# A mixture-of-experts kernel on one core: three partial sums instead of four, base rows loaded among the slots, and a row's transposes placed inside the prior row's products

## The chip, the core and the metric

The kernel runs on one core of one Trainium2 chip, as one launch. A core has engines with instruction queues of their own: TensorE (PE: matrix products and transposes; its weight loads are listed as PEld), VectorE (DVE), ScalarE (ACT), GpSimd (POOL) and SyncE (SP), whose queue here does nothing but issue DMAs. Each engine works through its queue in order and waits at an instruction whose inputs are not ready; what stands behind that instruction waits too. POOL issues the indirect DMAs, which scatter rows to addresses taken from an index. All DMAs share 16 DMA engines. TensorE's clock is granted: the profile gives it as a share of full speed, 0.50 or 1.00 here.

The metric is the device time of one execution in microseconds, the median over some runs. Lower is better.

## The reference, cut to what matters

The input is `x` (4 rows of 512 tokens, 512 channels each), a second tensor of the same shape and a small condition vector. Two blocks are added to `x`, one after the other:

```
x = x + attn(cond(x, side))          # recurrent mix, layer norms, dense products
x = x + ffn(cond2(x, side))
```

The part that the change touches is the end of the second block, a mixture of 32 experts. Each of the 2,048 tokens picks 8 experts and has a weight for each:

```
x_lat = x @ fc1_w.T                              # 256 values a token
h = relu2(einsum('tl,eil->eti', x_lat, w1))      # relu, then squared
h = h * cw.T[:, :, None]                         # 0 where the expert isn't picked
y_lat = einsum('eti,eli->tl', h, w2)             # sum over the experts
routed = y_lat @ fc2_w.T
shared = relu2(x @ shared_up_w.T) @ shared_down_w.T
return shared + routed
```

The kernel doesn't multiply all tokens by all experts. It sorts tokens by expert, works on groups of tokens of one expert, and adds each token's result into a row of a partial sum.

## The kernel before, in words

**Stages.** From the start to about 745 us the kernel computes the two conditioned mixes, the attention-like block, the router and the shared expert for the four rows, `b` = 0 to 3. At the end of that stage `base_dram[b]` holds, for each row, everything but the routed experts (`x`, the first block and the shared expert), channels on partitions: 4 chunks of 128 channels by 512 tokens. `x_dram` holds the tokens sorted by expert: per entry 256 latent values, the 32 weights and the token's number.

From 745 to about 1047 us run the **slots**: pairs of 128 entries each. `PAIRS` is 80; the first `SURE` = 74 always run, the rest under a condition, and in the profiled execution they do not run. The first `MIXED` = 16 pairs may hold two different experts, all later pairs hold 256 entries of one expert. For each pair, `fetch(i)` (L1068 to L1078) loads the entries with a DMA of SP, up to six pairs ahead; `slots(i, xg)` (L1117) transposes them on TensorE (`xt_ps`), multiplies by the expert's two matrices (`h_ps`, `y_ps`), scales by the token's weight on VectorE (`yo`, L1149) and adds the 128 x 256 results into DRAM with an indirect DMA that accumulates (L1151). Four arrays `sum_dram[0..3]` take these additions in turn, `(2 * i + j) % SUMS` for half `j` of pair `i`; two scatters into one array wait for each other. Entries that fill up a pair have weight 0 and go to spare rows behind row 2,047 of the array. The arrays are cleared by SP at 149 to 228 us from a block of zeros (`clear_sum`, L915 to L921), and the filling entries are laid out by `clear_tails` (L767).

From 1047 us to the end runs the **tail** (L1181 to L1219). For each row `b`:

- SP loads the row's part of each sum array (L1197), with token `t * 128 + p` on partition `p`, in runs of 1 KB;
- VectorE adds the four parts (L1203, three additions);
- TensorE transposes the result, eight 128 x 128 blocks into one PSUM tile `lt` (L1207);
- ScalarE copies it to SBUF as `yl` (L1211);
- TensorE multiplies by `fc2` in two halves, `j` = 0 and 1, four products each (L99), which the trace shows as eight matmuls;
- after each half VectorE adds the base (L1218), and SP stores the half to the output (L1219).

**What sets the order.** Each engine's instructions are written by hand inside a `manual_schedule` block for the engines it names; outside such a block, and for other engines, a scheduler picks the order. In the slots only VectorE is in written order. In the tail of the kernel before, no engine is: the scheduler orders all of it. SP is in written order up to the slots only, so the loads of base rows 0 to 2 (L1188) and of `fc2` (L1183), though written behind the slots, may be placed by the scheduler among the fetches.

Of the kernel before, what the change touches and what calls it, by code (L numbers as in the profile page):

```python
# [29 lines left out]
F32 = mybir.dt.float32  # L30
# [19 lines left out]
SURE = 74  # L50
MIXED = 16
WIDTH = 256 + E + 1
SUMS = 4
EXP30 = math.exp(30.0)
UNIT = NC * T

# [9 lines left out]
def model_kernel(ctx: ExitStack, tc: tile.TileContext, a: dict, out: bass.AP):  # L66
# [206 lines left out]

    x_dram = dram.tile([E * REGION + 3 * P, WIDTH], F32, tag="x_dram", name="x_dram")

    sum_dram = [dram.tile([ROWS + P, 256], F32, tag=f"sum{i}", name=f"sum{i}") for i in range(SUMS)]


    z_dram = [dram.tile([NC, P, T], F32, tag=f"z{b}", name=f"z{b}") for b in range(B)]
# [487 lines left out]
    def clear_tails():  # L767


        zeros = bp.tile([P, WIDTH], F32, tag="zeros", name="zeros")  # L770
        nc.vector.memset(zeros, 0.0)
        nc.gpsimd.iota(
            zeros[:, 256 + E : 257 + E], [[0, 1]], base=ROWS, channel_multiplier=1,
            allow_small_or_imprecise_dtypes=True,
        )
        for i in range(3):

            if i < 2:
                spare = x_dram[E * REGION : E * REGION + 2 * P, :].rearrange("(p j) n -> j p n", j=2)[i]
            else:  # L780
                spare = x_dram[E * REGION + 2 * P :, :]
            s = nc.gpsimd.dma_start(spare, zeros)
            tc.declare_no_dep(s.ins, group="scatter", reason="no two write one row")
            tc.add_to_no_dep_group("scatter", s.ins)
        yield
        ps = acc_tile()
        nc.tensor.matmul(ps[:1, 0, :E], lhsT=ones[:, 0:1], rhs=seen, start=True, stop=True)
        tail = bp.tile([1, E], F32, tag="tail", name="tail")
        nc.vector.tensor_tensor(tail, ps[:1, 0, :E], region[:1, :], ALU.add)
        ends = bp.tile([1, E], mybir.dt.int32, tag="ends", name="ends")  # L790
        nc.vector.tensor_scalar(ends, tail, -1.0, None, ALU.add)
        yield
        for e in range(E):
            _, (row,) = nc.values_load_multi_w_load_instructions(
                ends[0:1, e : e + 1], engines=[mybir.EngineType.SP], min_val=0, max_val=E * REGION,
                skip_runtime_bounds_check_because="a region has room for every row and a slot's tail",
            )
            s = nc.sync.dma_start(x_dram[bass.ds(row, P), :], zeros)
            tc.declare_no_dep(s.ins, group="scatter", reason="no two write one row but with zeros")
            tc.add_to_no_dep_group("scatter", s.ins)  # L800
            if e % 4 == 3:
                yield
# [112 lines left out]
    def clear_sum(i, j):  # L915

        s = sum_dram[i]
        if j < 2:
            nc.sync.dma_start(s[j * ROWS // 2 : (j + 1) * ROWS // 2, :].rearrange("(p r) n -> p (r n)", p=P), zero)
        else:  # L920
            nc.sync.dma_start(s[ROWS:, :], zero[:, :256])  # L921

    sums = iter([(i, j) for j in range(3) for i in range(SUMS)])

# [124 lines left out]
    with (  # L1049
# [19 lines left out]
        def fetch(i):  # L1069
            xg = ep.tile([P, 2, WIDTH], F32, tag="xg", name="xg", bufs=6)  # L1070
            rows = of_pair(2, i, ET.SP, E * REGION)
            if i < MIXED:
                for j, row in enumerate(rows):
                    nc.sync.dma_start(xg[:, j, :], x_dram[bass.ds(row, P), :])
            else:

                nc.sync.dma_start(xg, x_dram[bass.ds(rows[0], 2 * P), :].rearrange("(p j) n -> p j n", j=2))
            return xg  # L1078
# [37 lines left out]
        def slots(i, xg):  # L1116
            ps = turn(xg, "xt_ps")  # L1117
            xt = tile4("xt", [2, 2, P])
            if i < MIXED:
                nc.vector.tensor_copy(xt, ps)  # L1120
            else:
                nc.scalar.copy(xt, ps)

                w1 = tile4("w1", [2, 256])
                o = of_pair(0, i, ET.Activation, (E - 1) * (UNIT // 2))[0]
                nc.scalar.copy(w1.rearrange("p k n -> p (k n)"), big[:, bass.ds(o, 512)])  # L1126
            yield
            at = of_pair(0, i, ET.PE, (E - 1) * (UNIT // 2))
            h = tile4("ht", [2, 2, P])
            if i < MIXED:  # L1130
                ps = rows_times(xt, at, 0, "h_ps")
                r = tile4("hr", [2, 256])
                nc.scalar.activation(r, ps, AF.Relu)
                yield
                ps = turn(r, "ht_ps")
                nc.scalar.activation(h, ps, AF.Square)
            else:
                ps = inner(xt, w1)
                r = tile4("hr", [2, 256])
                nc.scalar.activation(r, ps.rearrange("p m j r -> p m (j r)"), AF.Relu)  # L1140
                yield
                nc.vector.tensor_tensor(h.rearrange("p m j r -> p m (j r)"), r, r, ALU.mult)  # L1142
            yield
            ps = rows_times(h, at, 1, "y_ps")
            y = tile4("yo", [2, 256], bufs=6)
            index = ep.tile([P, 2], mybir.dt.uint32, tag="index", name="index", bufs=9)
            nc.vector.tensor_copy(index, xg[:, :, 256 + E])
            for j, column in enumerate(of_pair(1, i, ET.DVE, 256 + E - 1)):
                nc.vector.tensor_scalar(y[:, j, :], ps[:, j, :], xg[:, j, bass.ds(column, 1)], None, ALU.mult)  # L1149

                nc.gpsimd.indirect_dma_start(  # L1151
                    out=sum_dram[(2 * i + j) % SUMS][:, :],
                    out_offset=bass.IndirectOffsetOnAxis(ap=index[:, j : j + 1], axis=0),
                    in_=y[:, j, :], in_offset=None,
                    bounds_check=ROWS + P - 1, compute_op=ALU.add,
                )
            yield

        def pairs(first, end):

            live = []
            with tc.manual_schedule(engines={ET.DVE}):
                for i in range(first, end + 3):
                    if i < end:
                        live.append(slots(i, fetch(i)))
                    for s in live:
                        next(s, None)
                    if len(live) > 3:
                        live.pop(0)
# [11 lines left out]

        fc2 = tile4("fc2", [2, C], bufs=1)
        nc.sync.dma_start(fc2, a["fc2"])  # L1183
        base = []
        for b in range(B):
            base.append(tile4(f"base{b}", [NC, T], bufs=1) if b + 1 < B else chunked(views(13, UNIT, 1)[0]))
            if b + 1 < B:
                nc.sync.dma_start(base[b], base_dram[b][:, :, :].rearrange("c p t -> p c t"))  # L1188
        got = Ring([v.rearrange("p (t n) -> p t n", t=NT) for v in views(1, NT * 256, 4 * SUMS)])
        lat_t = Ring([chunked(v, 2) for v in views(10, 2 * T, 2)])  # L1190
        res_ring = Ring([chunked(v, 2) for v in views(11, 2 * T, 4)])
        with tc.tile_pool(name="fpsum", bufs=2, space=bass.MemoryType.PSUM, reuse_waits="tile") as fps:
            for b in range(B):
                parts = []
                for s in sum_dram:
                    g = got()
                    nc.sync.dma_start(g, s[b * T : (b + 1) * T, :].rearrange("(t p) n -> p t n", p=P))  # L1197
                    parts.append(g)
                if b + 1 == B:
                    nc.sync.dma_start(base[b], base_dram[b][:, :, :].rearrange("c p t -> p c t"))  # L1200
                while len(parts) > 1:
                    for i in range(len(parts) // 2):
                        nc.vector.tensor_tensor(parts[i], parts[i], parts.pop(), ALU.add)  # L1203
                ps = fps.tile([P, 2, T], F32, tag="lt", name="lt")
                for t in range(NT):
                    for k in range(2):
                        nc.tensor.transpose(  # L1207
                            ps[:, k, t * P : (t + 1) * P], parts[0][:, t, k * P : (k + 1) * P], ident
                        )
                yl = lat_t()  # L1210
                nc.scalar.copy(yl, ps)  # L1211
                for j in range(2):
                    ps = fps.tile([P, 2, T], F32, tag="ps", name="ps")
                    for i in range(2):
                        o = (2 * j + i) * P
                        product(ps[:, i, :], lambda k: fc2[:, k, o : o + P], lambda k: yl[:, k, :], 2)
                    res = res_ring()
                    nc.vector.tensor_tensor(res, base[b][:, 2 * j : 2 * j + 2, :], ps, ALU.add)  # L1218
                    nc.sync.dma_start(out[b, 2 * j : 2 * j + 2].rearrange("c p t -> p c t"), res)  # L1219


# [40 lines left out]
```

## Time and profile before

| What | Value |
|---|---|
| median of 3 runs | 1114.19 us (1112.89 to 1116.45) |
| profiled execution, its own time | 1110.92 us |
| span of the profiled execution | 1109.2 us |
| mean granted TensorE clock | 0.983 |
| busy share: PE, DVE, ACT, POOL | 92%, 61%, 42%, 37% |
| scatters into the sums (L1151) | 148, mean 1610 ns on POOL, 4.0 us from issue to landing |
| loads of the sums (L1197) | 16 of 512 KB, 7.7 us from issue to landing |

The page divides the span into 40 slices of 27.7 us and gives a digit for the busy share of each, so the stages can be told apart in it. The timeline lists instructions in order of time: start, length, engine, line, operation, what is written and read, shapes, count, and in brackets how long the engine was idle before and what ended that. A time is counted from the start of the span. A "mean ns of one" is the time an instruction was in work; matmuls overlap, so the distance between two starts is the better measure for a row of them.

### The profile page before, as it was taken

How to read it: one execution, taken by the hardware profiler on the slowest of the kernel's cores; microseconds unless marked ns; L12 is line 12 of the kernel's file. 1: busy time of each engine (PE TensorE's matmuls, PEld its weight loads, DVE VectorE, ACT ScalarE, POOL GpSimd, SP SyncE). 2: the span in 40 equal slices, each digit the busy share in tenths (PEclk: the TensorE clock that was granted, in tenths of full speed). 3: DMA queues.
4: the chain of work that ended last, by engine and by line, in shares of the span. 5: the costliest groups of instructions: out<-in, count | busy, mean ns of one | idle time of the engine just before them, and what ended most of it. 6: DMA issues, size and time to landing. Idle time of an engine off the chain costs nothing.

```text
span 1109.2 us, 11550 instructions
## 1 busy us (share of the span) xinstructions
PE 1020.3 (92%) x3284; PEld 587.8 (53%) x3284; DVE 678.5 (61%) x1196; ACT 469.2 (42%) x671; POOL 408.3 (37%) x350
## 2 busy tenths in 40 slices
PE   3479899999999999999999999999999999999657
PEld 0134344344444444544454544448888888888523
DVE  7999799999896897439548622114434443333343
ACT  5555764865664655345235220303234444444100
POOL 3000000000001000436567635505777888888700
PEclk9989999999999999999999999999999999999869
DMA  3705384767347326754898859977988888888695
GB/s 131 274 29 209 114 246 164 306 175 228 132 100 241 146 104 184 253 141 131 257 332 276 258 184 291 284 231 183 202 137 143 143 142 144 144 148 148 68 287 205
DMA packets 105913, 208.41 MB, mean 188 GB/s; under 512 B 10837, under 2 KB 55385, under 8 KB 101177
## 3 DMA queue, kind: packets, MB, share of 16 engines
q1 hardware_dynamic: 71576, 152.07, 41.3%
q0 software_dynamic: 33728, 54.53, 27.3%
q10 hardware_dynamic: 544, 1.05, 0.2%
q8 instruction: 29, 0.48, 0.2%
q14 instruction: 36, 0.29, 0.1%
HBM read 126.87 MB, written 84.94 MB: 191 GB/s over the span
## 4 chain that ended last, share of the span: by engine, by line
PE 49%; DVE 25%; DMA 8%; issue 7%; ACT 6%; POOL 3%; SPq 0%; DVEq 0%; POOLq 0%; ACTq 0%
PE ps L99 17%; PE y_ps L1099 11%; PE h_ps L1110 9%; PE ps L500 6%; PE xt_ps L1088 3%; POOL x_dram L683 2%; PE h_ps L1099 2%; DMA big<-base 2%; DVE big L369 2%; DVE side L353 2%; DMA base<-big 2%; DVE big L353 2%; DVE side L369 2%; DVE big L465 2%; DMA sum<-yo,index 2%
## 5 line engine op out<-in xcount | busy, mean ns | idle before, releaser
L500 PE MATMUL ps<-big 128*128 128x512 f32 x896 | 392.6, 598 | 18.4 <-DVE big L465 7.9
L500 PEld LDWEIGHTS ps<-big 128*128 128x128 f32 x896 | 170.9, 192 | 236.4 <-issue 211.6
L1151 POOL DMA_INDIRECT sum<-yo,index x148 | 238.3, 1610 | 96.9 <-DVE yo L1149 73.0
L1149 DVE TENSOR_SCALAR yo<-y_ps,xg 128x256 f32<-128x256 f32 x148 | 64.8, 480 | 149.0 <-PE y_ps L1099 149.0
L683 POOL DMA_INDIRECT x_dram<-lat,index x128 | 139.5, 1090 | 42.6 <-issue 33.2
L1099 PE MATMUL y_ps<-big,ht 128*128 x592 | 140.3, 380 | 1.6 <-DVE ht L1142 1.6
L536 POOL DMA_DIRECT2D base<-big x8 | 10.6, 1323 | 313.6 <-DVE big L530 194.2
L1099 PEld LDWEIGHTS y_ps<-big,ht 128*128 128x128 f32 x592 | 106.8, 190 | 13.6 <-DVE ht L1142 2.2
L99 PE MATMUL ps<-big,sw 128*128 128x512 f32 x256 | 112.0, 593 | 0.2 <-DVE big L754 0.2
L1110 PE MATMUL h_ps<-xt,w 128*128 128x256 f32 x464 | 109.6, 379 | 0.0
L1110 PEld LDWEIGHTS h_ps<-xt,w 128*128 128x128 f32 x464 | 88.2, 190 | 11.8
L1140 ACT ACTIVATE hr<-h_ps 128x512 f32<-128x512 f32 x58 | 34.6, 597 | 132.0 <-PE h_ps L1110 132.0
L99 PEld LDWEIGHTS ps<-big,sw 128*128 128x128 f32 x256 | 48.4, 190 | 59.2 <-issue 57.6
L461 ACT ACTIVATE big<-big,vec,prior_g 128x511 f32<-128x511 f32 x80 | 58.4, 802 | 27.8 <-DVE big L454 27.8
L374 ACT ACTIVATE side<-side,tiny 128x512 f32<-128x512 f32 x32 | 23.1, 721 | 103.6 <-DVE side L371 103.5
L99 PE MATMUL ps<-sh,sw 128*128 128x512 f32 x128 | 56.7, 595 | 0.9 <-ACT sh L743 0.9
L465 DVE SCALAR_TENSOR_TENSOR big<-big,own_g 128x512 f32<-128x512 f32 x80 | 55.8, 749 | 0.3
L754 DVE TENSOR_TENSOR big<-big,ps 128x1024 f32<-128x1024 f32 x10 | 12.2, 1220 | 60.3 <-PE ps L99 36.6
L1126 ACT COPY w<-big 128x512 f32 x58 | 36.1, 622 | 28.3 <-DVE xt L1120 27.8
L369 DVE TENSOR_TENSOR_SCAN side<-decay,side 128x512 f32<-128x512 f32 x32 | 38.9, 1217 | 14.1 <-ACT side L354 14.1
L1088 PE MATMUL xt_ps<-ident,xg 128*128 128x128 f32 x296 | 44.3, 273 | 0.0
L1088 PEld LDWEIGHTS xt_ps<-ident,xg 128*128 128x128 f32 x296 | 36.9, 141 | 7.7 <-issue 0.5
(236 smaller groups left out, 1267.6 us busy)
## 6 DMA issues: line engine op xcount, KB each, us to landing
xg<-x_dram SPq DMA_DIRECT2D x58, 289.0 KB, 3.1
big<-in_w SPq DMA_DIRECT2D x32, 512.0 KB, 9.0
ekx<-side SPq DMA_DIRECT2D x16, 512.0 KB, 3.5
base<-big POOLq DMA_DIRECT2D x8, 1024.0 KB, 9.5
sum<-big SPq DMA_DIRECT2D x8, 1024.0 KB, 9.3
side<-ekx SPq DMA_DIRECT2D x16, 512.0 KB, 6.2
big<-sum SPq DMA_DIRECT2D x16, 512.0 KB, 7.7
side<-in_side SPq DMA_DIRECT2D x22, 256.0 KB, 6.6
```

The lines of the kernel that those rows point to most:

```text
L99: done[0] = nc.tensor.matmul(dst, lhsT=lhs(k), rhs=rhs(k), start=(k == 0), stop=(k == n - 1))
L353: nc.vector.tensor_tensor_scan(f, decb, data, 0.0, ALU.mult, ALU.add)
L369: nc.vector.tensor_tensor_scan(f[:, ::-1], decb, f[:, ::-1], 0.0, ALU.mult, ALU.add)
L461: nc.scalar.activation(m[:, c, 1:], xc[:, c, : T - 1], AF.Identity, bias=col(f"L0_attn_{which}_b", c), scale=prior_g[mu][:, c : c + 1],)
L465: nc.vector.scalar_tensor_tensor(m[:, c, :], xc[:, c, :], own_g[mu][:, c : c + 1], m[:, c, :], ALU.mult, ALU.add)
L500: done[0] = nc.tensor.matmul(ps[:, i, :], lhsT=w[:, k, f * P : (f + 1) * P], rhs=m[:, k, :], start=(k == 0), stop=(k == NC - 1),)
L683: s = nc.gpsimd.indirect_dma_start(out=x_dram[:, :], out_offset=bass.IndirectOffsetOnAxis(ap=index[:, i : i + 1], axis=0), in_=lats[:, t, ...
L1088: nc.tensor.transpose(ps[:, k, j, :], src[:, j, k * P : (k + 1) * P], ident)
L1099: nc.tensor.matmul(ps[:, j, :], lhsT=src[:, k, j, :], rhs=weights(at[j], of, k), start=(k == 0), stop=(k == 1),)
L1110: nc.tensor.matmul(ps[:, m, :, :], lhsT=w[:, k, m * P : (m + 1) * P], rhs=src[:, k, :, :], start=(k == 0), stop=(k == 1),)
L1149: nc.vector.tensor_scalar(y[:, j, :], ps[:, j, :], xg[:, j, bass.ds(column, 1)], None, ALU.mult)
L1151: nc.gpsimd.indirect_dma_start(out=sum_dram[(2 * i + j) % SUMS][:, :], out_offset=bass.IndirectOffsetOnAxis(ap=index[:, j : j + 1], axis=0 ...
```

## The change

Five things are changed.

- `SUMS` goes from 4 to 3. In the mixed pairs the halves still take the arrays in turn. From pair 16 on, both halves of pair `i` go to array `i % 3`, and the two scatters of one pair no longer wait for each other, since they hold different tokens of one expert. So that filling entries of one pair never meet in one row, the spare area of each array grows from 128 to 256 rows, and one of the spare blocks of entries gets row numbers 128 higher (`other`).
- The base rows are loaded in halves (512 KB each) by `load_base`, which is called among the pairs: seven halves there, the eighth with the loads of the sums.
- The sums are loaded with four tokens per partition: token `p * 4 + t` on partition `p`, one run of 4 KB per partition. All loads of all rows are written ahead of the arithmetic. ScalarE's copy puts the tokens back in order: it writes with a step of four elements.
- The tail's arithmetic is in a `manual_schedule` block for TensorE and VectorE. Additions, transposes and copy of a row are in `turned(b)`, which is called for row `b + 1` between the two halves of row `b`.
- The very last output half is added and stored in two pieces.

The diff, cut to its core:

```diff
-SUMS = 4
+SUMS = 3
...
-    sum_dram = [dram.tile([ROWS + P, 256], F32, tag=f"sum{i}", name=f"sum{i}") for i in range(SUMS)]
+    sum_dram = [dram.tile([ROWS + 2 * P, 256], F32, tag=f"sum{i}", name=f"sum{i}") for i in range(SUMS)]
...
+        other = bp.tile([P, 1], F32, tag="other", name="other")
+        nc.gpsimd.iota(
+            other, [[0, 1]], base=ROWS + P, channel_multiplier=1, allow_small_or_imprecise_dtypes=True,
+        )
...
-            s = nc.gpsimd.dma_start(spare, zeros)
...
+            parts = [(spare, zeros)]
+            if i == 1:
+                parts = [(spare[:, : 256 + E], zeros[:, : 256 + E]), (spare[:, 256 + E :], other)]
+            for dst, src in parts:
+                s = nc.gpsimd.dma_start(dst, src)
...
-            nc.sync.dma_start(s[ROWS:, :], zero[:, :256])
+            nc.sync.dma_start(s[ROWS:, :].rearrange("(p r) n -> p (r n)", p=P), zero[:, :512])
...
-                nc.gpsimd.indirect_dma_start(
-                    out=sum_dram[(2 * i + j) % SUMS][:, :],
+                s = nc.gpsimd.indirect_dma_start(
+                    out=sum_dram[(2 * i + j if i < MIXED else i) % SUMS][:, :],
...
+                if i >= MIXED:
+                    tc.declare_no_dep(s.ins, group=f"pair{i}", reason="rows of one expert")
+                    tc.add_to_no_dep_group(f"pair{i}", s.ins)
...
+        base = [[None, None] for _ in range(B)]
+        early = [(b, j) for b in range(B) for j in range(2)]
+
+        def load_base(b, j):
+
+            late = (b, j) == (B - 1, 1)
+            base[b][j] = chunked(views(13, 2 * T, 1)[0], 2) if late else tile4(f"base{b}{j}", [2, T], bufs=1)
+            nc.sync.dma_start(base[b][j], base_dram[b][halves[j]].rearrange("c p t -> p c t"))
...
+                    if i > MIXED and i % 4 == 0 and early:
+                        load_base(*early.pop(0)) if len(early) > 1 else None
...
-                    nc.sync.dma_start(g, s[b * T : (b + 1) * T, :].rearrange("(t p) n -> p t n", p=P))
+                    nc.sync.dma_start(g, s[b * T : (b + 1) * T, :].rearrange("(p t) n -> p t n", t=NT))
                     parts.append(g)
                 if b + 1 == B:
-                    nc.sync.dma_start(base[b], base_dram[b][:, :, :].rearrange("c p t -> p c t"))
+                    load_base(b, 1)
+
+            def turned(b):
+
+                parts = rows[b]
                 while len(parts) > 1:
                     for i in range(len(parts) // 2):
                         nc.vector.tensor_tensor(parts[i], parts[i], parts.pop(), ALU.add)
...
                 yl = lat_t()
-                nc.scalar.copy(yl, ps)
...
+                nc.scalar.copy(
+                    yl.rearrange("q k (p t) -> q k t p", t=NT), ps.rearrange("q k (t p) -> q k t p", t=NT)
+                )
+                return yl
+
+            with tc.manual_schedule(engines={ET.PE, ET.DVE}):
+                coming = turned(0)
+                for b in range(B):
+                    yl = coming
+                    for j in range(2):
+                        if j == 1 and b + 1 < B:
+                            coming = turned(b + 1)
+                        ps = fps.tile([P, 2, T], F32, tag="ps", name="ps")
+                        for i in range(2):
+                            o = (2 * j + i) * P
+                            product(ps[:, i, :], lambda k: fc2[:, k, o : o + P], lambda k: yl[:, k, :], 2)
+                        res = res_ring()
+
+                        for s in ((0, 1), (1, 2)) if (b, j) == (B - 1, 1) else ((0, 2),):
+                            s = slice(*s)
+                            nc.vector.tensor_tensor(res[:, s, :], base[b][j][:, s, :], ps[:, s, :], ALU.add)
+                            o = slice(2 * j + s.start, 2 * j + s.stop)
+                            nc.sync.dma_start(out[b, o].rearrange("c p t -> p c t"), res[:, s, :])
```

## The prediction

> **What bounds the kernel now.** I read the slices first, to see where TensorE is not full; then the timeline of the slots and of the tail; then the windows around the tail, for the clock; last the DMA issues.
>
> ```profile
> PE   3479899999999999999999999999999999999657
> PEclk9989999999999999999999999999999999999869
> ```
>
> TensorE is busy nine tenths or more from slice 6 to slice 37, and its clock is below nine tenths only in slice 3 and in slices 38 and 39. In the slots (745 to 1047 us) the timeline repeats a pair every 3.89 us with TensorE never idle: 220.00 us busy in 820 to 1040. No other engine's saving counts there. What remains is the tail:
>
> ```profile
> 1048.77 1.56 POOL L1151 DMA_INDIRECT sum<-yo,index  x1 [0.30 <-issue]
> 1053.81 12.96 SPq L1197 DMA_DIRECT2D big<-sum  x12
> 1060.70 1.22 DVE L1203 TENSOR_TENSOR big<-big 128x1024 f32<-128x1024 f32 x1 [14.59 <-DMA big<-sum]
> 1062.09 2.48 DVE L1203 TENSOR_TENSOR big<-big 128x1024 f32<-128x1024 f32 x2 [0.17 <-DMA big<-sum]
> 1064.72 1.94 PE L1207 MATMUL lt<-ident,big 128*128 128x128 f32 x8 [19.52 <-DVE big L1203]
> 1067.82 8.85 PE L99 MATMUL ps<-big,fc 128*128 128x512 f32 x16 [1.16 <-ACT big L1211]
> ...
> 1087.81 7.13 PE L99 MATMUL ps<-big,fc 128*128 128x512 f32 x16 [1.16 <-ACT big L1211]
> ...
> 1094.78 1.04 PE L1207 MATMUL lt<-ident,big 128*128 128x128 f32 x8
> ...
> 1095.91 1.01 ACT L1211 COPY big<-lt 128x1024 f32<-128x1024 f32 x1 [8.15 <-PE lt L1207]
> ...
> 1096.98 7.13 PE L99 MATMUL ps<-big,fc 128*128 128x512 f32 x16 [1.16 <-ACT big L1211]
> ...
> 1100.72 1.22 DVE L1218 TENSOR_TENSOR big<-big,ps 128x1024 f32<-128x1024 f32 x1 [4.51 <-PE ps L99]
> ...
> 1104.15 1.22 DVE L1218 TENSOR_TENSOR big<-big,ps 128x1024 f32<-128x1024 f32 x1 [2.21 <-PE ps L99]
> ```
>
> The reader is to see a head, a rhythm and an end. The head runs from the last scatter to the first transposes. The rhythm is one row per 9.17 us (1087.81 to 1096.98): 6.97 of products, 1.13 of transposes, 1.01 of ScalarE's copy, 0.06 to start. DVE's sums of the next row lie beside the products, ahead of the output adds, so TensorE waits only for the copy. The end is the last add, its store and the tail of the span (1104.15 to 1109.2).
>
> The third reading is the clock:
>
> ```profile
> 1040.60:1044.00 3.40, 1.83 (x9) 1.29 (x8) 1.55 (x4) 0.00 (x0) 2.79 (x3) 1.00 0.56 54
> 1044.00:1047.40 3.40, 1.20 (x6) 0.72 (x4) 0.88 (x2) 0.00 (x0) 2.79 (x3) 1.00 0.68 77
> 1047.40:1064.50 17.10, 0.00 (x0) 0.00 (x0) 3.60 (x3) 0.00 (x0) 2.62 (x2) 0.50 0.80 208
> 1064.50:1067.90 3.40, 2.02 (x9) 1.65 (x9) 1.29 (x2) 1.01 (x1) 0.00 (x0) 0.50 1.09 349
> 1067.90:1071.30 3.40, 3.40 (x4) 1.43 (x5) 2.46 (x3) 0.00 (x0) 0.00 (x0) 0.50 1.09 348
> 1071.30:1104.10 32.80, 29.39 (x85) 13.78 (x83) 15.54 (x13) 3.04 (x3) 0.00 (x0) 1.00 0.68 230
> ```
>
> Columns: the stretch, its length, busy time of PE, PEld, DVE, ACT, POOL, granted clock, DMA share, GB/s. The clock moves in steps of 3.41 us. A step with 1.83 us of matmuls (54%) leaves it full; one with 1.20 us (35%) is followed by half clock; 59% at half clock doesn't bring it back, a full step does.
>
> **The change, part by part.**
>
> *Base rows.* In the trace the scheduler already loads rows 0 to 2 (L1188, 1 MB each) at 766, 770 and 774 us, during the slots; only row 3's load is late (1084.06), and its first user waits for TensorE at 1100.72, not for it. So nothing is removed. In the compiled order of the changed kernel, seven halves go ahead of the seventh to ninth fetch on SP's queue. Fetches behind them wait at most 3.5 MB, some 10 us at the 348 GB/s of the tail. The seventh fetch is needed six pairs after the first, at 4.33 us each (760.25 to 764.58 on POOL). Cost: 0; without that cover, up to 10 us, once.
>
> *Three sums in the slots.* From pair 16 on a scatter waits for the scatters of three pairs before, at least 9.8 us after their issue (three pairs of 3.89 less the 1.86 between a pair's two); before it was 7.8. Scatters land 4.0 us after issue (median; 8.0 at most), so the wait is covered. In the 16 mixed pairs the distance falls from four scatters to three, some 6.2 us (4.33 + 1.87): covered at the median, short by 1.8 at the longest. GpSimd idles 0.9 us per mixed pair and `yo` has six buffers, so TensorE doesn't see it. POOL's backlog at the end of the slots is 1.2 us (the last product's first half is scaled by 1045.7, so two scatters of 1.56 with 0.30 between could end at 1049.1, and end at 1050.3). It may go or stay: minus 1.2 to 0, and I take 0. The spare-row edit adds one iota and one small DMA on POOL's queue before its first base add at 140 us, with idle time behind it: 0. Nine clears instead of twelve on SP: 0, for TensorE waits on VectorE there; half a microsecond either way stays in the range.
>
> *The head.* Four loads of 512 KB become three, in 4 KB runs instead of 1 KB. The first load landed 3.74 us after its issue, the next ones some 1.48 us apart (seen in 1063.63 and 1065.10, the landings of the fifth and sixth), so the third landed near 1060.6 and the fourth near 1062.0: the two DVE starts above. The longer runs cost a little less: 4 KB packets took 173 ns on an engine (the ekx loads), 16 engines, so 1.38 us a load. Third load: 1053.81 + 3.65 + 2 x 1.38 = 1060.2. Two dependent adds are 2.48, plus 0.1 and 0.12 to start: transposes at 1062.9 instead of 1064.7. Gain **1.8**.
>
> *The row turned between the halves.* This is the step that decides. The block has VectorE and TensorE in written order, and the code writes product, output add of half 0, then `turned(b + 1)` with its sums, then product of half 1. So on VectorE the next row's two sums stand behind an add that waits for the product of half 0, and on TensorE the transposes that wait for these sums stand ahead of half 1's product. TensorE now waits inside every row but the last. From a product's start: 3.74 to its output add (1096.98 to 1100.72), 1.22 for the add, 2.48 for the two sums, 0.15 to the transposes, 0.86 for eight of them (four take 0.43 from 833.34 to the next product at 833.77), 3.43 for half 1 (sixteen matmuls take 6.86, 704.05 to 710.91): 11.9 us to the next row's product. ScalarE's copy and its 0.06 are now beside half 1's product; without that cover they would be 1.1 more. Three rows: 3 x (11.9 - 9.17) = **8.1 lost**. What disappears per row is the copy gap of 1.1 and one sum that was hidden anyway; what is new is 4.2 us of idle TensorE.
>
> *The clock in these gaps.* A gap of 4.2 us, however it lies on steps of 3.41, puts at least 2.1 idle us into one of them: 39% busy or less. The row above dropped at 35% and held at 54%, so I take a drop in each of the three gaps. Then half clock lasts until a step is nearly full. Placing the gap at every phase of the step, 1.7 to 3.1 us of work time is lost per drop, 2.1 in the mean: 3 x 2.1 = **6.3 lost** (an estimate from the rows above). The Trainium skill ("TensorE: Matmul & The Clock Gate", What's actually happening) is milder: the clock halves after an idle window of about 3.4 us, free-running. A gap of 4.2 contains a whole one in about a quarter of the placings: less than one drop, 2 us in all. By the rule the sum below would be +7, by the row +11.6; I follow the row, since the 35% step was no idle window and dropped.
>
> *The strided copy.* ScalarE writes `yl` with a step of four elements. No row shows such a write; the nearest is the same copy, contiguous, 1.01 us. The skill's page "SBUF — State Buffer" (Door 1) speaks against it: accesses that move to a new 16-byte line pay a penalty, and a step of four fp32 values moves every time. It gives no time. Bounds: 1.01 and twice that. Only row 0's copy is on the path; the others have 3.43 us of product over them. I take 0, and 1.0 as the other end.
>
> *The end.* The last output add is split. The first half can start after the first two of four products, so the piece behind the last product is 128x512: 0.68 us (L1142's row) instead of 1.22, and its store is 256 KB instead of 512 (2.79 us to landing before, perhaps 0.5 less). Gain **1.0**.
>
> Sum: 8.1 + 6.3 - 1.8 - 1.0 = **+11.6 us**. On the profiled execution (1109.2 span, 1110.92 with what lies around it) that gives 1122.5. The three runs shown have a median of 1114.19, 3.3 above the profiled one; on it, **1125.8**.
>
> **Rivals.**
> *The clock holds in the gaps.* For it: the skill's rule; against: the 35% step. 8.1 - 1.8 - 1.0 = +5.3: 1119.5, or 1121.5 with one drop.
> *More is late.* The strided copy at double time (+1.0), a scatter wait in the mixed pairs (+1.8) or three drops at the costly phase (+3): 1128 to 1131.
> *Faster.* The turn is truly hidden: if the sums of the next row ended before half 0's product, a row would take 6.86 + 0.86 = 7.7 and the sum would be 3 x (7.7 - 9.17) - 1.8 - 1.0 = -7.2: 1107. The point is whether two sums fit ahead of the output add on VectorE; data would be there (six loads by 1064.4). The written order speaks against it.
> *The change doesn't do what it says* holds for the base rows, as shown; it is inside the main case.
>
> **Chances.** Main case 0.66 (its own range 1122 to 1129), clock holds 0.19, more is late 0.11, hidden 0.04. About 0.3% (3.3 us) is what a measurement can tell from no change. Same takes a small part of the second case, where POOL's backlog goes too (8.1 - 2.8 - 1.2 = +4.1) and the runs spread: 0.05. Range 1118.5 to 1130.
>
> **What would show it.** Between halves of a row, TensorE idle about 4 us, released by the sums; VectorE's order output add, sum, sum; the clock at 0.5 after these gaps; first transposes near 1063; slots at 3.89 us per pair. It is wrong if the sums of row 1 start before half 0's output add, or if the slots' pace moves.

## The result, and the profile after

The changed kernel takes **1125.44 us** (median of 4 runs, 1123.18 to 1126.34); the kernel before, run beside it, takes 1113.54 (4 runs, 1111.98 to 1116.45). The ratio is 1.0096 with a 95% interval of 1.0078 to 1.0115: 11.9 us slower, where 11.6 was forecast.

The profiled execution of the changed kernel took 1125.58 us, its span is 1123.8, its mean clock 0.978. These are the slices of its page, first TensorE's busy share and then the granted clock:

```profile
PE   3579899999999999999999999999999999999267
PEclk9989999999999999999999999999999999999779
```

The last three slices tell it: TensorE is busy two, six and seven tenths there (six, five and seven before), and the clock is at seven, seven and nine (eight, six and nine before). The timeline shows why, from TensorE's last product of the slots on:

```profile
1044.96 1.99 PE L1108 MATMUL y_ps<-big,ht 128*128 x8 [1.57 <-DVE ht L1151]
...
1052.39 1.56 POOL L1161 DMA_INDIRECT sum<-yo,index  x1 [0.31 <-issue]
1057.19 7.90 SPq L1220 DMA_DIRECT2D big<-sum  x12
1063.60 2.48 DVE L1230 TENSOR_TENSOR big<-big 128x1024 f32<-128x1024 f32 x2 [15.73 <-DMA big<-sum]
...
1066.23 1.94 PE L1234 MATMUL lt<-ident,big 128*128 128x128 f32 x8 [19.28 <-DVE big L1230]
1068.27 1.95 ACT L1238 COPY big<-lt 128x1024 f32<-128x1024 f32 x1 [26.08 <-PE lt L1234]
1070.27 6.18 PE L99 MATMUL ps<-big,fc 128*128 128x512 f32 x8 [2.10 <-ACT big L1238]
1076.49 1.22 DVE L1259 TENSOR_TENSOR big<-base,ps 128x1024 f32<-128x1024 f32 x1 [10.41 <-PE ps L99]
1077.63 2.48 DVE L1230 TENSOR_TENSOR big<-big 128x1024 f32<-128x1024 f32 x2
...
1080.25 1.94 PE L1234 MATMUL lt<-ident,big 128*128 128x128 f32 x8 [3.80 <-DVE big L1230]
1081.98 8.80 PE L99 MATMUL ps<-big,fc 128*128 128x512 f32 x16
...
1090.82 1.22 DVE L1259 TENSOR_TENSOR big<-base,ps 128x1024 f32<-128x1024 f32 x1 [2.21 <-PE ps L99]
1091.96 2.48 DVE L1230 TENSOR_TENSOR big<-big 128x1024 f32<-128x1024 f32 x2
1094.49 1.09 PE L1234 MATMUL lt<-ident,big 128*128 128x128 f32 x8 [3.71 <-DVE big L1230]
...
1107.86 1.09 PE L1234 MATMUL lt<-ident,big 128*128 128x128 f32 x8 [3.71 <-DVE big L1230]
...
1115.86 1.22 DVE L1259 TENSOR_TENSOR big<-base,ps 128x1024 f32<-128x1024 f32 x1 [2.21 <-PE ps L99]
1119.29 1.29 DVE L1259 TENSOR_TENSOR big<-big,ps 128x512 f32<-128x512 f32 x2 [2.21 <-PE ps L99]
```

Read the 1076.49 line and the two below it: output add, then the next row's two sums, then TensorE's transposes, which waited 3.80 us for them. The same triple stands at 1090.82 and before 1107.86. The output adds of the four first halves start at 1076.49, 1090.82, 1104.18 and 1115.86: distances of 14.33, 13.36 and 11.67, where before all three were near 9.15.

Two of the three rows are longer than the third, though the instructions are the same. The windows of the clock's steps say why (columns as in the prediction; the last three numbers are granted clock, DMA share and GB/s):

```profile
1075.30:1078.70 3.40, 1.15 (x3) 0.19 (x1) 2.21 (x2) 0.00 (x0) 0.00 (x0) 1.00 0.12 43
1078.70:1082.10 3.40, 1.85 (x9) 1.88 (x10) 1.37 (x2) 0.00 (x0) 0.00 (x0) 0.50 0.40 149
1092.40:1095.80 3.40, 1.31 (x9) 1.12 (x10) 2.00 (x2) 0.13 (x1) 0.00 (x0) 1.00 0.41 154
1095.80:1099.20 3.40, 3.40 (x5) 1.35 (x4) 0.00 (x0) 1.85 (x1) 0.00 (x0) 0.50 0.02 5
1102.60:1106.00 3.40, 1.55 (x4) 0.38 (x2) 1.81 (x2) 0.00 (x0) 0.00 (x0) 1.00 0.41 154
1106.00:1109.40 3.40, 1.54 (x10) 1.31 (x11) 1.77 (x2) 0.36 (x1) 0.00 (x0) 1.00 0.41 154
1109.40:1112.80 3.40, 3.40 (x9) 1.49 (x9) 0.38 (x1) 1.64 (x1) 0.00 (x0) 1.00 0.00 0
```

The first gap leaves its step 34% busy (1.15 of 3.40) and the next step runs at half clock; the second leaves 39% and the clock drops again. The third gap falls across a boundary: 46% and 45%, and the clock holds.

The two spans differ by 14.6 us. The table goes stage by stage. Of the kernel before, these are the last slot product and the first output add; the other lines stand in the prediction:

```profile
1043.20 2.00 PE L1099 MATMUL y_ps<-big,ht 128*128 x8 [1.57 <-DVE ht L1142]
...
1073.28 1.22 DVE L1218 TENSOR_TENSOR big<-base,ps 128x1024 f32<-128x1024 f32 x1 [2.61 <-PE ps L99]
```

| stage | before, us | after, us | difference |
|---|---|---|---|
| span's start to the end of the last slot product | 1045.20 | 1046.95 | +1.75 |
| from there to the first load of the sums | 8.61 | 10.24 | +1.63 |
| first load to first transposes | 10.91 | 9.04 | -1.87 |
| first transposes to first product | 3.10 | 4.04 | +0.94 |
| first product to its output add | 5.46 | 6.22 | +0.76 |
| that add to the last row's first add | 27.44 | 39.37 | +11.93 |
| last row's first add to the span's end | 8.43 | 7.95 | -0.48 |

The first row is not shown to be the change's. The difference is there at the first pair's transposes (745.25 before, 747.19 after). Ahead of them the diff touches only the clears of the sums and the entries that fill up pairs, and in experiments that share all of this with the changed kernel the transposes start at 745.36, 747.03 and 749.02, so executions scatter by more than the difference. The other rows sum to 12.9. The medians differ by 11.9; the profiled execution of before was 2.6 us below its median, and the profiles do not say in which stage.

The second row was not foreseen, and has a cause of its own. GpSimd's part of the timeline, in the mixed pairs and around pair 16:

```profile
762.00 1.56 POOL L1161 DMA_INDIRECT sum<-yo,index  x1 [0.85 <-DVE yo L1158]
...
766.96 1.55 POOL L1161 DMA_INDIRECT sum<-yo,index  x1 [3.40 <-DMA sum<-yo,index]
...
824.51 1.56 POOL L1161 DMA_INDIRECT sum<-yo,index  x1 [0.30 <-issue]
...
830.35 1.56 POOL L1161 DMA_INDIRECT sum<-yo,index  x1 [4.29 <-DVE yo L1158]
832.21 1.56 POOL L1161 DMA_INDIRECT sum<-yo,index  x1 [0.30 <-issue]
```

The scatter at 824.51 is the last mixed one, number 31, and goes to array 31 % 3 = 1. The next is pair 16's first, and goes to array 16 % 3 = 1. So it stands behind a scatter that was issued one place earlier, which landed at 828.32. GpSimd sat idle for 4.29 us; the VectorE instruction named as releaser had ended at 826.26, so the likely cause is the other wait, the landing (an experiment below tests it). The wait at 766.96 is of the kind that the prediction had priced, and that backlog was gone by pair 10. The one at pair 16 was not: a pair's first scatter then started 4.1 us after its data was ready, and still 3.1 at the last pair (1.2 before).

### The profile page after: what moved, and what is told of

It is laid out like the page before. It is cut to its first block, busy times and chain, and to the rows that moved or that the text cites. A ratio compares the mean times of both kernels' runs of the same rounds, so it can differ in the third digit from the quotient of the medians.

```text
span 1123.8 us, 11489 instructions
## 1 busy us (share of the span) xinstructions
PE 1025.7 (91%) x3284; PEld 589.2 (52%) x3284; DVE 668.8 (60%) x1193; ACT 473.6 (42%) x671; POOL 407.6 (36%) x352
## 5 line engine op out<-in xcount | busy, mean ns | idle before, releaser
L1119 PEld LDWEIGHTS h_ps<-xt,w 128*128 128x128 f32 x464 | 88.1, 190 | 11.9
```

The source lines that it names most:

```text
L1119: nc.tensor.matmul(ps[:, m, :, :], lhsT=w[:, k, m * P : (m + 1) * P], rhs=src[:, k, :, :], start=(k == 0), stop=(k == 1),)
```

## The experiments

The theory at this point: the written order costs 3 x 11.67 - 27.44 = 7.6 us, the two drops of the clock 39.37 - 3 x 11.67 = 4.4, pair 16's array 1.6, the strided copy 0.9, and the head and the end give 2.35 back. The rivals: the gaps come from late data, not from the order; the clock is slower for another reason than the gaps; the late scatters come from three arrays as such, or from the base loads. Four kernels ran on one chip, beside 11 runs of the kernel before (median 1113.40, 1111.19 to 1116.82).

**The sums ahead of the output adds.** Only VectorE's written order is changed: each row's sums stand before the adds that they were queued behind.

```diff
-            def turned(b):
+            def summed(b):
                 parts = rows[b]
                 while len(parts) > 1:
...
+            def turned(b):
+                parts = rows[b]
...
+                summed(0)
+                summed(1)
                 coming = turned(0)
...
                             nc.sync.dma_start(out[b, o].rearrange("c p t -> p c t"), res[:, s, :])
+                        if j == 0 and b + 2 < B:
+                            summed(b + 2)
```

> Only VectorE's order in the tail is moved: the two sums of row 1 stand ahead of row 0's first output add, those of rows 2 and 3 one half of a row earlier than in the changed kernel. Theory (the sums behind the output add make TensorE wait, and the gaps halve its clock): no gap at the transposes of rows 1 to 3; one row to the next in 7.7 us instead of 14.3, 13.4 and 11.7; first output add of row 0 to that of row 3 in 23 to 24 us instead of 39.4; clock full from the first product's end on; about 1109 us, 16 less than the changed kernel and 4 less than the kernel before. Rival (TensorE waits there for something else, such as the loads of the sums or ScalarE's strided copy of 2 us): gaps of 2 to 4 us remain at the transposes, and the time stays above 1118.

Measured: 1107.64 us (6 runs, 1106.94 to 1110.72), ratio to the kernel before 0.9948 (0.9933 to 0.9963). Its timeline between the halves of row 0:

```profile
1068.99 2.48 DVE L1230 TENSOR_TENSOR big<-big 128x1024 f32<-128x1024 f32 x2 [1.32 <-DMA big<-sum]
...
1071.89 5.82 PE L99 MATMUL ps<-big,fc 128*128 128x512 f32 x8 [2.14 <-ACT big L1242]
1077.54 1.04 PE L1238 MATMUL lt<-ident,big 128*128 128x128 f32 x8
1077.74 1.22 DVE L1265 TENSOR_TENSOR big<-base,ps 128x1024 f32<-128x1024 f32 x1 [6.27 <-PE ps L99]
1078.41 7.03 PE L99 MATMUL ps<-big,fc 128*128 128x512 f32 x16
...
1078.88 2.48 DVE L1230 TENSOR_TENSOR big<-big 128x1024 f32<-128x1024 f32 x2
```

Row 1's sums run at 1068.99, while row 0 is still being turned, so its transposes at 1077.54 follow the product with no bracket, that is with no idle time. A row takes 7.74 us three times, and the clock is full from 1076.2 on:

```profile
1076.20:1103.00 26.80, 26.80 (x82) 13.21 (x81) 13.27 (x11) 6.11 (x3) 0.00 (x0) 1.00 0.36 133
```

With nothing but this order changed, all gaps and drops between the rows are gone. The data was there, so the data rival falls. The turn between the halves is worth 27.44 - 3 x 7.74 = 4.2 us against the kernel before, if VectorE has the sums ready.

**The gap filled.** Half 1's product of each row but the last is computed once more, in the gap, and overwritten by the real one. The waits stay as they are; TensorE is busy in them.

```diff
-                        if j == 1 and b + 1 < B:
-                            coming = turned(b + 1)
                         ps = fps.tile([P, 2, T], F32, tag="ps", name="ps")
+                        if j == 1 and b + 1 < B:
+                            for i in range(2):
+                                o = (2 * j + i) * P
+                                product(ps[:, i, :], lambda k: fc2[:, k, o : o + P], lambda k: yl[:, k, :], 2)
+                            coming = turned(b + 1)
```

> The order of the changed kernel is kept; in each of the three gaps TensorE computes the product of half 1 once more, ahead of the transposes, into the PSUM tile that the real product then overwrites (eight matmuls, 3.4 us at full clock, inside the gap of 4.2). The order alone then costs what it did, but TensorE isn't idle. Theory that the clock drop is a part of its own: clock at full from the first products on, first output add of row 0 to that of row 3 in about 35 us (three rows of 11.7) instead of 39.4, so some 4 us faster than the changed kernel, about 1121. Rival (the slower rows come from the order alone, or from slower products for another reason): 39 us or more, time unchanged or longer by the added products.

Measured: 1119.2 us (6 runs, 1117.6 to 1120.46), ratio 1.0052 (1.0036 to 1.0067). Its windows, around the second gap and over all of the tail from where the clock is back:

```profile
1087.40:1090.80 3.40, 3.40 (x8) 1.14 (x6) 3.37 (x3) 0.00 (x0) 0.00 (x0) 1.00 0.40 150
1090.80:1094.20 3.40, 3.13 (x14) 1.94 (x15) 0.21 (x1) 1.95 (x1) 0.00 (x0) 1.00 0.06 17
1073.90:1107.00 33.10, 32.18 (x92) 15.01 (x92) 13.18 (x11) 5.98 (x3) 0.00 (x0) 1.00 0.26 97
```

The steps are now 92% busy or more and the clock stays at 1.00. The rows take 11.74, 11.67 and 11.67: 35.08 in all, 4.29 less than in the changed kernel. That is the clock's share, and 35.08 - 27.44 = 7.6 is the order's. The order and the waits are those of the changed kernel, so the clock fell because TensorE idled in them. Twenty-four more matmuls make the kernel faster than the changed one: they fit into gaps that were there anyway, and the clock stays up.

**Pair 16 to another array.** The first unmixed pair no longer meets the array of the scatter before it; three arrays and base loads stay.

```diff
-                    out=sum_dram[(2 * i + j if i < MIXED else i) % SUMS][:, :],
+                    out=sum_dram[(2 * i + j if i < MIXED else i + 1) % SUMS][:, :],
```

> Pairs 16 and later go to array (i + 1) % 3 instead of i % 3, so that pair 16 doesn't take the array that the scatter just before it went to. Theory (that one wait of 4.3 us at pair 16 gives GpSimd the backlog that it carries to the end, since it can make up only 0.17 us a pair): no wait at pair 16; the first scatter of the last pairs starts 0.7 to 1.2 us after its operand instead of 3.1; the last scatter ends some 2 us nearer to TensorE's last slot product (7.0 us behind it in the changed kernel, 5.1 before). Rival (the backlog comes from the waits for two scatters each, or from GpSimd's pace): 3 us as now. Too small for the total time to tell in one run.

Measured: one run, 1122.48 us. The timeline around pair 16, then the last slot product and the last scatter:

```profile
822.68 1.56 POOL L1161 DMA_INDIRECT sum<-yo,index  x1 [0.31 <-DMA sum<-yo,index]
824.84 2.02 POOL L1161 DMA_INDIRECT sum<-yo,index  x1 [0.60 <-DVE yo L1158]
827.16 1.56 POOL L1161 DMA_INDIRECT sum<-yo,index  x1 [0.30 <-issue]
...
1043.13 1.99 PE L1108 MATMUL y_ps<-big,ht 128*128 x8 [1.57 <-DVE ht L1151]
...
1048.70 1.56 POOL L1161 DMA_INDIRECT sum<-yo,index  x1 [0.30 <-issue]
```

Pair 16's first scatter starts after 0.60 us at 824.84, in place of 4.29. The last pair's scatter starts 1.2 us after its data, as in the kernel before, and the last scatter ends 5.14 us after the last slot product (7.00 in the changed kernel, 5.13 before). The three later kernels with this edit show the same 5.13 to 5.14; without it, the last scatter ends 6.99 to 8.86 us after the product (four profiles). So the backlog at the end came from this one meeting, not from three arrays as such nor from the base loads. Of the 3.1 us between the two profiled executions, 1.8 lie ahead of the first pair and are no gain of the edit; 1.8 lie between last product and first load and are; 0.5 the other way lies behind the first load.

**The tokens in rows of 128 again.** Loads in 1 KB runs and a contiguous copy, as before the change; all else as changed.

```diff
-                    nc.sync.dma_start(g, s[b * T : (b + 1) * T, :].rearrange("(p t) n -> p t n", t=NT))
+                    nc.sync.dma_start(g, s[b * T : (b + 1) * T, :].rearrange("(t p) n -> p t n", p=P))
...
-                nc.scalar.copy(
-                    yl.rearrange("q k (p t) -> q k t p", t=NT), ps.rearrange("q k (t p) -> q k t p", t=NT)
-                )
+                nc.scalar.copy(yl, ps)
```

> The sums are loaded with 1 KB runs again, token t * 128 + p on partition p, and ScalarE's copy is contiguous; all else as changed. Theory (the strided write doubles the copy): copies of 1.01 us instead of 1.95 to 2.00; last transposes of row 0 to its first product 1 us shorter; loads 1.48 us apart instead of 1.28, so row 0's sums start some 0.5 us later after the first load's issue. Rows 1 to 3 unchanged, since the copy lies beside half 1's product. Rival (the copy is slow because of the clock or of the DMAs beside it): stays near 2 us.

Measured: one run, 1125.26 us. Row 0's copy and what follows it in the timeline:

```profile
1068.75 1.01 ACT L1238 COPY big<-lt 128x1024 f32<-128x1024 f32 x1 [28.39 <-PE lt L1234]
1069.82 6.27 PE L99 MATMUL ps<-big,fc 128*128 128x512 f32 x8 [1.16 <-ACT big L1238]
```

The same copy takes 1.01 us instead of 1.95, so the step of four elements alone doubles it. Transposes to product is 3.10 again (4.04). The loads land 1.50 us apart instead of 1.28, and the head is 9.60 instead of 9.04. So four tokens per partition cost 0.94 on the path and bring 0.56: a net loss of 0.4, not the gain that the loads alone would suggest. The head is 8.82 to 9.14 in the three experiments above, so the loss is better put at 0.2 to 0.5. The total can't show it, since here GpSimd was 4.9 us late at the last pair (3.1 in the changed kernel) and the last scatter 1.9 later behind the last product.

Then the mends were put together, on a second chip, where the kernel before took 1122.75 us (11 runs, 1120.43 to 1123.06). That chip is slower for the same program, so only ratios on it are compared.

**Both mends:** the sums ahead, and pair 16's other array (the two edits above).

> The two mends together: VectorE's sums ahead of the output adds, and pair 16's scatters into another array than the one just written. If the two losses are apart from each other, the tail keeps its 7.74 us a row and no gap, GpSimd's last scatter ends about 5.1 us behind TensorE's last slot product instead of 7.0, and the time is some 1.9 us below the one with the sums ahead: about 1105.7. Rival (the backlog at the end depends on chance, or the loads then wait for something else): 1107.6 as with the sums ahead alone.

Measured: 1114.87 us (6 runs, 1112.34 to 1118.51), ratio 0.9931 (0.9918 to 0.9945). The rows take 7.74 us, and the last scatter ends 5.14 us after the last product. The ratio's interval overlaps that of the sums ahead alone, so the total doesn't show the second mend; the trace does.

**The last product in two tiles:** both mends, and the last piece's product in a PSUM tile of its own, so that its neighbour's add needn't wait for it.

```diff
+                        last = (b, j) == (B - 1, 1)
                         ps = fps.tile([P, 2, T], F32, tag="ps", name="ps")
+                        own = [ps, fps.tile([P, 2, T], F32, tag="lt", name="lt") if last else ps]
...
-                            product(ps[:, i, :], lambda k: fc2[:, k, o : o + P], lambda k: yl[:, k, :], 2)
+                            product(own[i][:, i, :], lambda k: fc2[:, k, o : o + P], lambda k: yl[:, k, :], 2)
...
-                            nc.vector.tensor_tensor(res[:, s, :], base[b][j][:, s, :], ps[:, s, :], ALU.add)
+                            nc.vector.tensor_tensor(res[:, s, :], base[b][j][:, s, :], own[s.stop - 1][:, s, :], ALU.add)
```

> As with both mends, and the second piece of the very last half has a PSUM tile of its own (one that is free by then), so that the add of the first piece doesn't wait for the whole half. Theory (both pieces waited for the last product because they shared a tile): first piece's add starts 1.7 us before the second's instead of 0.6, only one add of 0.68 us lies behind the last product, and from the output add of row 3's half 0 to the end of the span it takes 7.3 us instead of 7.95. Rival (the end is set by the store's landing, which doesn't move): 7.95 as now. About 1105.1; not told apart from the two mends by the total.

Measured: 1114.39 us (6 runs, 1112.28 to 1117.71), ratio 0.9932 (0.9918 to 0.9947). The end of its timeline:

```profile
1108.63 1.88 PE L99 MATMUL lt<-big,fc 128*128 128x512 f32 x4
1108.84 0.69 DVE L1267 TENSOR_TENSOR big<-big,ps 128x512 f32<-128x512 f32 x1 [0.50 <-PE ps L99]
1110.55 0.69 DVE L1267 TENSOR_TENSOR big<-big,lt 128x512 f32<-128x512 f32 x1 [1.03 <-PE lt L99]
```

The two adds stand 1.71 us apart, the first beside the last four matmuls; in the changed kernel they came 0.60 apart, both after the whole product (the line at 1119.29, x2). From the last row's first add to the end is 7.26 instead of 7.95. That 0.7 is too small for the total to show.

**The same with tokens in rows:** the mends, the two tiles, and the loads and copy of the fourth experiment.

> As the one with the own tile at the end, and with the sums loaded in 1 KB runs and a contiguous copy. From its single parts: 0.94 us less from the first transposes to the first product, 0.56 us more from the first load to the first transposes, so 0.4 us less in all: about 1104.7, the best of these. Rival (with no gaps left the slower loads of 1.48 us each hold up the sums of rows 1 to 3, which must now be ready sooner): gaps before the transposes of row 1, and no gain.

Measured: 1112.78 us (5 runs, 1111.86 to 1116.5), ratio 0.9916 (0.9903 to 0.9929). It has the lowest ratio of all, and is faster than both kernels: against the kernel before directly, and with that against the changed one, whose ratio is 1.0096. The copy takes 1.01 us, first load to first transposes 9.71, a row 7.74, the end 7.26. Its lead over the other two of this chip lies inside their intervals, and their heads, with 4 KB runs, are 9.93 and 8.88: what the tokens bring in all is not shown here.

The early base loads were not undone by themselves. What is known of them comes from the traces.

## Why the prediction was right

The forecast of 1125.8 met 1125.44, and the mechanism is the forecast one: the next row's sums queue behind an output add, TensorE idles for them, and the clock falls in the gaps. That the number came within 0.4 us is luck. The order and the clock were put 2.5 us too high; pair 16's wait, the strided copy and the first product, all put at nothing, and the end came out 3.8 us worse.

- **Base rows, 0: right for TensorE.** Seven halves are issued at 755 to 763 us, and TensorE is busy 220.00 us in 820 to 1040, as before. Beside them scatters landed as late as 8.56 us (8.01 before), and with three arrays mixed pairs 2 to 9 were up to 3.8 us late, more than the 1.8 that was said; `yo` covered it, for TensorE did not wait. How much of this lateness the loads cause was not separated.
- **Three sums, 0: wrong by 1.6.** The step weighed the distance in the mixed pairs and the distance from pair 16 on, and left out the seam between them, where the two formulas for the array meet at a distance of one. "I take 0" held for TensorE; the end of the slots paid, because GpSimd's last scatter is what the tail waits for. The edit of pair 16's array shows it.
- **Head, -1.8: right** (-1.87). The loads landed 1.28 us apart (1.38 said): a 4 KB packet of the ekx transfers took 159 ns in the median in the trace of before, not 173, and eight make 1.27.
- **Order, +8.1: 7.6.** The row is 11.67 at full clock (11.9 said), TensorE's gap 3.71 to 3.80 (4.2 said).
- **Clock, +6.3: 4.3**, and this is the term that the shorter gap mis-sized. With 4.2 us one step could not be busier than 39%, and the prediction took that for a drop, though its rows left open everything between 35% and 54%; the limit turned out to lie between 39% and 42%. With 3.71 a gap that straddles two steps evenly leaves both at 46%, and one of three did. That is a matter of where the gap falls; in the two experiments that keep the gaps one of three held, too. Per drop it is 2.15, as the 2.1 of the estimate. The choice between row and rule was right: both drops came after steps that were 34% and 39% busy. The rule of the Trainium skill ("TensorE: Matmul & The Clock Gate", What's actually happening) asks for a whole idle window of about 3.4 us, and neither step was one.
- **Strided copy, 0: wrong by 0.94.** The value was the other end of the stated bound: 1.95 to 2.00 us against 1.01. The Trainium skill's page "SBUF — State Buffer" (Door 1) was quoted for a penalty at each new 16-byte line; it goes on to name four fp32 values as how far one can stride for free, which the prediction left out. For this copy the measurement bears out the penalty and not the free stride. As said, only row 0's copy is on the path.
- **End, -1.0: -0.5.** "The first half can start after the first two of four products" was wrong: both pieces read one PSUM tile and waited for its whole product. The own tile shows that this was the reason. What was gained is the smaller store: 2.10 us to landing instead of 2.79.

In sum, 11.6 was said; 7.6 + 4.3 + 1.6 + 0.9 - 1.9 - 0.5 = 12.0 came, with 0.8 more in the first product. There the clock came back 5.0 us after the product's start, 3.5 before, and half of the 1.5 between is that 0.8. The rival "clock holds" was put at +5.3; the filled gap, which is that case, measured +5.8 (4.0 to 7.5, by its interval). The rival "faster", -7.2 if the sums ran ahead, is what the reordered kernels show: -5.8 (-7.5 to -4.1) with pair 16's wait still in, 0.9931 with it mended.

## What to carry to other kernels

In a block with a written order, ask of every instruction that a product waits for: what stands ahead of it on its own engine, and does that wait for a product too? If so, write it earlier, since moving work "between two halves" hides it only if its inputs are made before the first half ends. Where a formula for buffers changes in the middle of a loop, check the distance across the seam, and when an idle gap on TensorE can't be removed, count what the clock makes of it as a cost of its own.

## What the runs showed of the hardware

- **The clock's threshold is sharp.** In all nine profiles, every stretch of one clock between two changes is a whole number of steps of 3.41 us. Full clock was lost after each step with 39% of matmuls or less (the busiest 0.37, 0.38 and 0.39) and kept after each step with 42% or more (the emptiest 0.42, 0.44, 0.45, 0.46). Coming back took a nearly full step: 66% and, in the kernel with both mends, 82% (1078.14 to 1081.55) were not enough; 88% in the one with two tiles (1078.28 to 1081.69) was.
- **A stride doubles ScalarE's copy:** 128x1024 fp32 written with a step of four elements took 1.95 to 2.07 us, contiguous 1.01.
- **GpSimd's lag settles at levels.** From pair 16 on two scatters with their gaps need 3.72 us of a pair's 3.89, so a backlog should drain by 0.17 per pair. It does, until the lag is 2.7, and then stays: every other scatter takes 1.73 us instead of 1.56, and the pair just fills 3.89. Other runs stayed at 0.7 or at 4.6, so the levels lie about half a pair apart. What holds it there was not found, nor why pair 16's scatter started 2.0 us after the landing that it waited for.
- **Two chips differ by 0.8%** on the same program (1113.40 and 1122.75 us), more than any single term of the sum. In the profiles the first pair's transposes start at 756.43 to 757.51 us on the second, 745.36 to 749.02 on the first; the slots then take the same time on both.
